# Attention scores as float32 products on 32-row groups instead of split operands stacked through DRAM

## The chip, the cores and the metric

The kernel runs on one core of a Trainium2 chip. Its metric is the device time of one execution in microseconds. The engines of the core have short names in the profile: PE is TensorE's matmul, PEld its weight load, DVE is VectorE, ACT is ScalarE, POOL is GpSimd, and SP is SyncE, whose queue issues the DMAs. A matmul multiplies a stationary operand (loaded by a weight load, up to 128 rows by 128 columns) by a moving operand of up to 512 columns and writes into PSUM, which has eight banks of 512 float32 columns for each of 128 partitions.

## The reference

Four layers follow each other on x (2 sequences of 1024 tokens, 512 wide), each added to its input: a gated recurrence, a feed-forward layer with ternary weights, an attention, and the same feed-forward layer again. The change lies in the attention. Cut to what matters, it is:

```python
B, T, D = x.shape                      # 2, 1024, 512
d = D // H                             # H = 16 heads of 32
q1 = _split_heads(x @ Wq1, H)
q2 = _split_heads(x @ Wq2, H)
k = _split_heads(x @ Wk, H)
v = _split_heads(x @ Wv, H)
q = jnp.concatenate([q1, q2], axis=1)
k2 = jnp.repeat(k, 2, axis=1)
v2 = jnp.repeat(v, 2, axis=1)
scores = jnp.einsum('bhqd,bhkd->bhqk', q, k2) * scale
scores = jnp.where(causal, scores, jnp.finfo(scores.dtype).min)
p = jax.nn.softmax(scores, axis=-1)
y = jnp.einsum('bhqk,bhkd->bhqd', p, v2)
y1, y2 = (y[:, :H], y[:, H:])
lam = jax.nn.sigmoid(x @ Wlam).transpose(0, 2, 1)[..., None]
y = y1 - lam * y2
```

There are 32 query heads, each two of which share a key head. A score is a product over only 32 numbers. The queries of a later token see only earlier ones.

## The kernel before

The attention of a sequence is worked off in **pairs** (line 665): two key heads (e = 0, 1) with one of their two query heads each (the parity `par`). The list `pairs` runs over the sequence b, the group g of four key heads, the half p of the group, and the parity; there are 32 pairs. `project` (L708 to L738) makes, for one group and one kind (kinds 0 and 1: queries of the two parities, kind 2: keys), the product of 512 tokens with the weights, 128 rows = 4 heads x 32. ScalarE writes its rounded high part into `parts` (L724, L728), VectorE the low part (L725, L729), both float32r, and eight DMAs write them to a scratch tensor in DRAM (L738). `load_stacks` reads, two pairs ahead, what a head needs: `ks` has the keys' high part twice and low part twice, `qs` has high, low, high, low, each 32 rows, so that one fp32r matmul over 128 rows adds up all four partial products of a score (L750, L754).

Every score is made twice. `maxima_step` (L785) makes scores with queries on the partitions (tile `s`, L798); VectorE adds the causal mask on the diagonal (L804) and takes the negated maximum of each row (L808). `split_maxima` splits the maxima into three bf16 pieces on GpSimd, and `turn_maxima` turns them with four transposes (tile `mt`, L836) and a VectorE copy (L838). `weights_step` (L843) makes scores again with keys on the partitions (tile `t`, L858), adds the maxima by a bf16 matmul of three rows (L865), and ScalarE takes the exponential into `pr` (L873); on the diagonal GpSimd zeroes what is masked (L876). `weigh` multiplies the weights with the values and a column of ones (tile `y`, L895), in float32, head 0 to the partitions 0 to 63 and head 1 to 64 to 127.

A pair has six steps. TensorE's order is written out by hand in the loop at the end of the attention: in each step first the four products `t` of two (query block, key tile) units and two heads, and their four maxima products; then `y` of the two units of the step before; then what `beside` lists for that step (transposes of the maxima, projections of the next group, normalisation, the output products); and then the step of maxima of the next pair. The units' widths are 512, 384, 256, 128 columns for the first query block and four times 512, then 512, 384, 256, 128 for the second. The banks come from a ring of seven (`ring_bank`), taken in order; a bank is free once its readers of seven banks ago are done: ScalarE for `t`, VectorE for `s`, both for `pq` of a projection, VectorE for `mt`. The list `max_banks` says which products of `s` share a bank: 20 banks a pair, in steps of 4, 4, 3, 3, 3 and 3.

Before the first pair the queries, keys and stacks of its group are made, then `lambdas` and the first maxima with the products of the values between them.

Of the kernel before, what the change touches and what calls it, by code (L numbers as in the profile page):

```python
# [10 lines left out]
F32 = mybir.dt.float32  # L11
F32R = mybir.dt.float32r
# [30 lines left out]
def kernel(  # L43
# [571 lines left out]
    with ExitStack() as s:  # L615
# [5 lines left out]
        ps_ring = s.enter_context(  # L621
            tc.tile_pool(name="b_ring", bufs=7, space=bass.MemoryType.PSUM, reuse_waits="tile")
        )
        kd = s.enter_context(tc.tile_pool(name="b_dram", bufs=2, space=bass.MemoryType.DRAM))

        def ring_bank(name, dtype=F32):
            return ps_ring.tile(
# [39 lines left out]
            (b, g, p, par)  # L667
            for b in range(NT // SEQ) for g in range(NG) for p in range(2) for par in range(2)
        ]
        scratch, stacks, nmax, lams, totals, shares, factors = {}, {}, {}, {}, {}, {}, {}  # L670

        def load_weights(b, g):
            w = b_b.tile([P, NKC, 3 * P], F32, tag="w_qk", name=f"w_qk{b}_{g}")
# [37 lines left out]
        def project(b, g, kind, e, w):  # L711


            n = f"{b}_{g}_{kind}"
            po = ring_bank(f"pq{n}_{e}")
            for k in range(NKC):
                nc.tensor.matmul(  # L717
                    po, w[:, k, ts(kind, P)], xts[b][:, k, ts(e, BLK)],
                    start=(k == 0), stop=(k == NKC - 1),
                )  # L720
            parts = b_p.tile([P, 2, BLK], F32R, tag="parts", name=f"parts{n}_{e}", bufs=2)
            hi, lo = parts[:, 0, :], parts[:, 1, :]
            if kind == 2:
                nc.scalar.copy(hi, po)  # L724
                nc.vector.tensor_sub(lo, po, hi.bitcast(F32))  # L725
            else:
                scale = 1.0 / math.sqrt(HD)
                nc.scalar.mul(hi, po, scale)  # L728
                nc.vector.scalar_tensor_tensor(  # L729
                    lo, po, scale, hi.bitcast(F32), ALU.mult, ALU.subtract  # L730
                )
            if e == 0:

                scratch[b, g, kind] = kd.tile([4, 2, HD, SEQ], F32, tag=f"sc{kind}", name=f"sc{n}")
            sc = scratch[b, g, kind]
            for r in range(2):
                for i in range(4):
                    nc.sync.dma_start(  # L738
                        out=sc[i, r, :, ts(e, BLK)], in_=parts[ts(i, HD), r, :].bitcast(F32)
                    )  # L740

        def load_stack(b, g, kind, i):


            n = f"{b}_{g}_{kind}_{i}"
            sc = scratch[b, g, kind]
            if kind == 2:
                st = b_a.tile([P, SEQ], F32R, tag="ks", name=f"ks{n}", bufs=4)
                for r in range(4):
                    nc.sync.dma_start(out=st[ts(r, HD)].bitcast(F32), in_=sc[i, r // 2])  # L750
            else:
                st = b_d.tile([P, SEQ], F32R, tag="qs", name=f"qs{n}", bufs=6)
                for r in range(2):
                    nc.sync.dma_start(  # L754
                        out=st[ts(r, 2 * HD)].bitcast(F32),
                        in_=sc[i].rearrange("e d n -> (e d) n"),
                    )
            stacks[b, g, kind, i] = st

        def load_stacks(pair):  # L760
            b, g, p, par = pair
            for e in range(2):
                if par == 0:
                    load_stack(b, g, 2, 2 * p + e)
                load_stack(b, g, par, 2 * p + e)

        def operands(pair, e):
            b, g, p, par = pair
            i = 2 * p + e
            return stacks[b, g, 2, i], stacks[b, g, par, i], 4 * g + i  # L770

        def name(pair):
            return "_".join(map(str, pair))

        max_banks = [
            [(0, 0, 128, (0, 1)), (1, 0, 256, (0, 1)), (2, 0, 384, (0,)), (2, 0, 384, (1,))],
            [(j, 0, 512, (e,)) for j in (3, 4) for e in range(2)],
            [(4, 512, 128, (0, 1)), (5, 0, 512, (0,)), (5, 0, 512, (1,))],  # L780
            [(5, 512, 256, (0, 1)), (6, 0, 512, (0,)), (6, 0, 512, (1,))],
            [(6, 512, 384, (0,)), (6, 512, 384, (1,)), (7, 0, 512, (0,))],
            [(7, 0, 512, (1,)), (7, 512, 512, (0,)), (7, 512, 512, (1,))],
        ]

        def maxima_step(pair, step):


            if step == 0:
                nmax[pair] = b_a.tile(  # L790
                    [P, 2, NQ, 2], F32, tag="nmax", name=f"nmax{name(pair)}", bufs=2
                )
            for i, (j, first, nk, heads) in enumerate(max_banks[step]):
                po = ring_bank(f"s{name(pair)}_{step}_{i}")[:, : len(heads) * nk]
                po = po.rearrange("p (e n) -> p e n", n=nk)
                for x, e in enumerate(heads):
                    ks, qs, _ = operands(pair, e)
                    nc.tensor.matmul(  # L798
                        po[:, x, :], qs[:, ts(j, P)], ks[:, first : first + nk],
                        start=True, stop=True,  # L800
                    )
                if first + nk == (j + 1) * P:
                    diagonal = po[:, :, nk - P :]
                    nc.vector.tensor_tensor(  # L804
                        diagonal, diagonal,
                        causal.unsqueeze(1).to_broadcast([P, len(heads), P]), ALU.add,
                    )
                nc.vector.tensor_reduce(  # L808
                    nmax[pair][:, first // BLK, j, heads[0] : heads[-1] + 1], po,
                    AX.X, ALU.max, negate=True,  # L810
                )

        turned = {}
        n_maxima = [0]
# [29 lines left out]
        def weights_step(pair, step):  # L844

            made, banks = [], {}
            for u in (2 * step, 2 * step + 1):
                qb, kb = units[u]  # L850
                lo = max(0, kb - qb * QB) * P
                made.append((u, kb, lo, BLK - lo, kb >= qb * QB))
            for u, kb, lo, nq, _ in made:
                for e in range(2):
                    ks, qs, _ = operands(pair, e)
                    banks[u, e] = ring_bank(f"t{name(pair)}_{u}_{e}")
                    q0 = (qb + 1) * BLK - nq
                    nc.tensor.matmul(  # L858
                        banks[u, e][:, :nq], ks[:, ts(kb, P)], qs[:, q0 : q0 + nq],
                        start=True, stop=False,  # L860
                    )
            for i, (u, kb, lo, nq, _) in enumerate(made):
                for e in range(2):
                    rows = slice(64 * i + 32 * e, 64 * i + 32 * e + 3)
                    nc.tensor.matmul(  # L865
                        banks[u, e][:, :nq], ones[rows], turned[pair, qb][rows, lo:],
                        start=False, stop=True,
                    )
            steps = []
            for u, kb, lo, nq, diagonal in made:  # L870
                pr = b_a.tile([P, 2, BLK], F32, tag="pr", name=f"pr{name(pair)}_{u}", bufs=4)
                for e in range(2):
                    nc.scalar.activation(pr[:, e, :nq], banks[u, e][:, :nq], AF.Exp)  # L873
                if diagonal:

                    nc.gpsimd.affine_select(  # L876
                        out=pr[:, :, :P], in_=pr[:, :, :P], compare_op=ALU.is_ge, fill=0.0,
                        base=0, pattern=[[0, 2], [1, P]], channel_multiplier=-1,
                    )
                steps.append((pair, u, pr))  # L880
            return steps

        def weigh(pair, u, pr):
# [7 lines left out]
            y = outs[pair]  # L891
            last = kb == (qb + 1) * QB - 1
            for e in range(2):
                h = operands(pair, e)[2]
                nc.tensor.matmul(  # L895
                    y[64 * e : 64 * e + 64, lo:],
                    all_values[:, HV * (NH * kb + h) : HV * (NH * kb + h) + 64],
# [77 lines left out]
        for n, pair in enumerate(pairs):  # L975
            b, g, p, par = pair
            following = pairs[n + 1] if n + 1 < len(pairs) else None
            if following:
# [1 line left out]
                at(n, 3, turn_maxima, following, 0)  # L980
                at(n + 1, 0, split_maxima, following, 1)
                at(n + 1, 1, turn_maxima, following, 1)
            if n + 2 < len(pairs):
                at(n, 1, load_stacks, pairs[n + 2])

            nb, ng = divmod(4 * b + g + 1, NG)
            if p == 0 and nb < NT // SEQ:
                def part(kind, e, nb=nb, ng=ng):
                    return lambda: project(nb, ng, kind, e, held["w", nb, ng])
                if par == 0:  # L990
                    at(max(n - 1, 0), 0, lambda nb=nb, ng=ng: hold(("w", nb, ng), load_weights, nb, ng))
                    for t, kind, e in ((1, 2, 0), (2, 2, 1), (4, 0, 0), (5, 0, 1)):
                        at(n, t, part(kind, e))
                else:
                    for t, e in ((2, 0), (4, 1)):
                        at(n, t, part(1, e))

            if g == 2 and p == 1 and b + 1 < NT // SEQ:
                if par == 0:
                    at(n, 0, normal_stats, b + 1)  # L1000
                for t in range(4):
                    at(n, 1 + t, normalise, b + 1, 4 * par + t, ring_bank)
            if g == 3 and p == 1 and b + 1 < NT // SEQ:
                if par == 0:
                    at(n, 0, lambda b=b: hold(("v", b + 1), load_values, b + 1))
# [29 lines left out]
        for kind in (2, 0):  # L1035
            for e in range(2):
                project(0, 0, kind, e, w0)
        load_stacks(pairs[0])
        for e in range(2):
            project(0, 0, 1, e, w0)  # L1040
        load_stacks(pairs[1])
        lambdas(0)
        for step in range(STEPS):
            maxima_step(pairs[0], step)
# [98 lines left out]
```

## Time and profile before

| what | value |
|---|---|
| time before, median of 3 runs | 2176.9 us (2176.82 to 2177.41) |
| profiled execution, its own time | 2177.11 us |
| its span | 2175.3 us |
| granted TensorE clock, mean | 0.995 |
| matmul records and weight loads | 9072 each |
| L858 `t`, float32r, 768 records | 198.4 us busy, mean 357 ns |
| L798 `s`, float32r, 768 records | 206.9 us busy, mean 391 ns |
| L895 `y`, float32, 1536 records | 291.6 us busy, mean 501 ns |
| L717 `pq`, float32, 384 records | 175.8 us busy, mean 603 ns |
| DMA `sc<-parts` / `qs<-sc` / `ks<-sc` | 384 of 64 KB / 128 of 256 KB / 128 of 128 KB |

A float32 matmul stands in the trace as two records, a float32r or bf16 one as a single one. [...] a slot, from the start of one record to the start of the next, is the better measure of what a matmul costs TensorE. In a line of the timeline the columns are the start in us, the length from the first start to the last end in us, engine, line, operation, output <- inputs, the shape of the first record and the number of records; brackets give the idle time before it and what ended it.

### The profile page before, as it was taken

The numbers are of one execution on the slowest core, as the hardware profiler recorded it, in microseconds if no ns is written. First come the engines' busy times: TensorE is split into PE (matmuls) and PEld (weight loads), VectorE is DVE, ScalarE is ACT, GpSimd is POOL, SyncE is SP. The second block draws the span as 40 slices with busy tenths as digits, with TensorE's granted clock in tenths as the row PEclk, the third lists the DMA queues.
The fourth block names the chain that finished last, engine by engine and source line by source line (L and its number), as shares of the span: only waits on it lengthen the run. The fifth ranks groups of instructions, "written<-read, shape, count | busy, mean of one in ns | idle before, by whom it ended". The sixth has DMA issues, their size and how long they took to land.

```text
span 2175.3 us, 26073 instructions
## 1 busy us (share of the span) xinstructions
PE 2122.4 (98%) x9072; PEld 1273.5 (59%) x9072; DVE 1126.2 (52%) x2056; ACT 837.3 (38%) x1592; POOL 448.1 (21%) x808
## 2 busy tenths in 40 slices
PE   8999999999999999999999999999999999999998
PEld 3444444688888844555555454454545547888887
DVE  4767676533443235565656574565656763333322
ACT  4344343234334322343444332243434533343433
POOL 0312123122122220111111112121212221222222
PEclk9999999999999999999999999999999999999999
DMA  6111211600000144343434341244443223000000
GB/s 251 58 58 58 88 58 73 246 1 1 1 1 1 35 105 106 98 112 87 121 83 119 76 123 41 73 104 106 104 105 88 64 83 160 0 20 20 1 20 20
DMA packets 77874, 161.41 MB, mean 74 GB/s; under 512 B 19376, under 2 KB 27568, under 8 KB 77744
## 3 DMA queue, kind: packets, MB, share of 16 engines
q1 hardware_dynamic: 77744, 159.75, 25.1%
q8 instruction: 73, 1.20, 0.2%
q14 instruction: 57, 0.47, 0.1%
HBM read 109.08 MB, written 41.94 MB: 69 GB/s over the span
## 4 chain that ended last, share of the span: by engine, by line
PE 86%; DVE 4%; DMA 4%; ACT 2%; SPq 2%; issue 2%; POOL 0%; DVEq 0%; ACTq 0%; POOLq 0%
PE y L895 11%; PE g L511 11%; PE u L511 11%; PE f_out L532 11%; PE t L858 6%; PE s L798 5%; PE ag L260 5%; PE kv L260 5%; PE pq L717 4%; PE pq L260 3%; PE pv L689 3%; PE a_out L408 3%; PE b_out L956 2%; DMA qs<-sc 2%; PE t L865 2%
## 5 line engine op out<-in xcount | busy, mean ns | idle before, releaser
L873 ACT ACTIVATE pr<-t 128x512 f32<-128x512 f32 (+3 forms) x768 | 314.8, 497 | 368.6 <-PE t L865 364.8
L808 DVE TENSOR_REDUCE nmax<-s 128x1 f32<-128x512 f32 (+3 forms) x640 | 369.7, 627 | 54.6 <-PE s L798 54.5
L895 PE MATMUL y<-pr,val 128*64 128x512 f32 (+3 forms) x1536 | 291.6, 501 | 0.8 <-POOL maxima L827 0.8
L526 POOL TENSOR_TENSOR ssq<-ssq,sq 128x512 f32<-128x512 f32 x120 | 155.9, 1299 | 602.5 <-ACT sq L525 602.5
L517 DVE TENSOR_TENSOR h<-h,u 128x512 f32<-128x512 f32 x128 | 88.0, 688 | 362.5 <-PE u L511 356.4
L511 PE MATMUL g<-xs,w 128*128 128x512 f32 x1024 | 261.8, 397 | 0.9 <-ACT xs L461 0.7
L532 PE MATMUL f_out<-w,hs 128*128 128x512 f32 x1024 | 257.7, 394 | 0.3 <-DVE hs L520 0.3
L511 PE MATMUL u<-xs,w 128*128 128x512 f32 x1024 | 257.0, 393 | 0.0
L876 POOL TENSOR_SCALAR_AFFINE_SELECT pr<-pr 128x256 f32<-128x256 f32 x256 | 101.4, 408 | 593.6 <-ACT pr L873 593.3
L858 PE MATMUL t<-qs,ks 128*128 128x512 f32 (+3 forms) x768 | 198.4, 357 | 22.1 <-DVE parts L729 9.6
L511 PEld LDWEIGHTS u<-xs,w 128*128 128x128 f32 x1024 | 192.9, 188 | 43.6
L532 PEld LDWEIGHTS f_out<-w,hs 128*128 128x128 f32 x1024 | 191.6, 188 | 43.9 <-DVE hs L520 1.1
L804 DVE TENSOR_TENSOR s<-s,causal 128x128 f32<-128x128 f32 (+1 forms) x384 | 115.3, 336 | 195.3 <-PE s L798 195.3
L511 PEld LDWEIGHTS g<-xs,w 128*128 128x128 f32 x1024 | 190.5, 188 | 43.9 <-ACT xs L461 0.9
L798 PE MATMUL s<-ks,qs 128*128 128x512 f32 (+3 forms) x768 | 206.9, 391 | 6.2 <-DMA sc<-parts 3.9
L858 PEld LDWEIGHTS t<-qs,ks 128*128 128x128 f32 x768 | 139.2, 188 | 78.2 <-issue 20.8
L717 PE MATMUL pq<-b_xt,w_qk 128*128 128x512 f32 x384 | 175.8, 603 | 0.0
L519 ACT CAST hs<-h 128x512 fp32r<-128x512 f32 x128 | 79.4, 621 | 237.5 <-DVE h L517 237.5
L895 PEld LDWEIGHTS y<-pr,val 128*64 128x64 f32 x1536 | 93.3, 136 | 120.2 <-issue 86.1
L516 ACT ACTIVATE h<-g 128x512 f32<-128x512 f32 x128 | 76.6, 598 | 224.0 <-PE g L511 223.9
L798 PEld LDWEIGHTS s<-ks,qs 128*128 128x128 f32 x768 | 115.0, 190 | 69.4 <-issue 58.6
L520 DVE TENSOR_TENSOR hs<-h,hs 128x512 fp32r<-128x512 f32 x128 | 88.6, 692 | 83.1 <-ACT hs L519 83.1
(151 smaller groups left out, 2145.5 us busy)
## 6 DMA issues: line engine op xcount, KB each, us to landing
qs<-sc SPq DMA_DIRECT2D x128, 256.0 KB, 4.9
w<-w_kept SPq DMA_DIRECT2D x32, 768.0 KB, 8.9
sc<-parts SPq DMA_DIRECT2D x384, 64.0 KB, 1.7
ks<-sc SPq DMA_DIRECT2D x128, 128.0 KB, 4.0
w_kept<-w SPq DMA_DIRECT2D x16, 768.0 KB, 3.2
w<-in_w_gu_dram SPq DMA_DIRECT2D x32, 256.0 KB, 2.8
share<-ys SPq DMA_DIRECT2D x128, 64.0 KB, 2.0
w_in<-in_w_in_t_dram SPq DMA_DIRECT2D x5, 1024.0 KB, 11.0
```

Of the source, the lines that this page charges most:

```text
L260: nc.tensor.matmul(po, w[:, k, ts(c, P)], xt[:, k, :], start=(k == 0), stop=(k == NKC - 1))
L511: nc.tensor.matmul(po, ws[f][:, part, ts(k, P)], xs[:, e, k, :], start=(k == 0 and e == 0), stop=(k == NKC - 1 and e == 1),)
L526: nc.gpsimd.tensor_add(ssq, ssq, sq)
L532: nc.tensor.matmul(po[j], hp[:, e, ts(j, P)], ws[f][:, 2, :], start=(f == 0 and e == 0), stop=(f == NF - 1 and e == 1),)
L717: nc.tensor.matmul(po, w[:, k, ts(kind, P)], xts[b][:, k, ts(e, BLK)], start=(k == 0), stop=(k == NKC - 1),)
L798: nc.tensor.matmul(po[:, x, :], qs[:, ts(j, P)], ks[:, first : first + nk], start=True, stop=True,)
L804: nc.vector.tensor_tensor(diagonal, diagonal, causal.unsqueeze(1).to_broadcast([P, len(heads), P]), ALU.add,)
L808: nc.vector.tensor_reduce(nmax[pair][:, first // BLK, j, heads[0] : heads[-1] + 1], po, AX.X, ALU.max, negate=True,)
L858: nc.tensor.matmul(banks[u, e][:, :nq], ks[:, ts(kb, P)], qs[:, q0 : q0 + nq], start=True, stop=False,)
L873: nc.scalar.activation(pr[:, e, :nq], banks[u, e][:, :nq], AF.Exp)
L876: nc.gpsimd.affine_select(out=pr[:, :, :P], in_=pr[:, :, :P], compare_op=ALU.is_ge, fill=0.0, base=0, pattern=[[0, 2], [1, P]], channel_mu ...
L895: nc.tensor.matmul(y[64 * e : 64 * e + 64, lo:], all_values[:, HV * (NH * kb + h) : HV * (NH * kb + h) + 64], pr[:, e, : BLK - lo], start= ...
```

## The change

The split into high and low parts, the scratch in DRAM and the stacks go. `project` keeps what ScalarE writes, in full float32, in a tile `group` in SBUF with two copies of the 128 rows: copy 0 as it comes, and copy 1 with the two halves of 64 rows exchanged, written by two DMAs from SBUF to SBUF for each projection. A pair's two heads are one half of the rows in copy 0 and the other half in copy 1, so each head is there on two groups of 32 rows. `operands(pair, i, e)` gives head e on the rows 32 (2i + e). The score products become float32 matmuls over 32 rows: in `weights_step` unit i of the step uses the half i, so that the four products use four row groups; in `maxima_step` each bank belongs to one head and one row group, three banks of 512 columns a step (18 a pair), filled by one or two products. Reductions are one for a bank whose products are equally long, otherwise one for each product. The projections of the next group move to the steps 1, 3 and 5, three for each of two pairs (before: four and two), and the normalisations of the next sequence to the steps 1 and 3.

```diff
-        kd = s.enter_context(tc.tile_pool(name="b_dram", bufs=2, space=bass.MemoryType.DRAM))
...
-            parts = b_p.tile([P, 2, BLK], F32R, tag="parts", name=f"parts{n}_{e}", bufs=2)
-            hi, lo = parts[:, 0, :], parts[:, 1, :]
+            if e == 0:
+
+                pool = (b_d, b_a, b_p)[kind]
+                groups[b, g, kind] = pool.tile(
+                    [P, 2, SEQ], F32, tag=f"group{kind}", name=f"gr{n}", bufs=2
+                )
+            made = groups[b, g, kind][:, :, ts(e, BLK)]
             if kind == 2:
-                nc.scalar.copy(hi, po)
-                nc.vector.tensor_sub(lo, po, hi.bitcast(F32))
+                nc.scalar.copy(made[:, 0, :], po)
             else:
...
-            if e == 0:
-
-                scratch[b, g, kind] = kd.tile([4, 2, HD, SEQ], F32, tag=f"sc{kind}", name=f"sc{n}")
-            sc = scratch[b, g, kind]
-            for r in range(2):
-                for i in range(4):
-                    nc.sync.dma_start(
-                        out=sc[i, r, :, ts(e, BLK)], in_=parts[ts(i, HD), r, :].bitcast(F32)
-                    )
-
-        def load_stack(b, g, kind, i):
...
+                nc.scalar.mul(made[:, 0, :], po, 1.0 / math.sqrt(HD))
+            for i in range(2):
+                nc.sync.dma_start(out=made[ts(i, 64), 1, :], in_=made[ts(1 - i, 64), 0, :])
+
+        def operands(pair, i, e):
+
             b, g, p, par = pair
-            i = 2 * p + e
-            return stacks[b, g, 2, i], stacks[b, g, par, i], 4 * g + i
+            rows = ts(2 * i + e, HD)
+            return (groups[b, g, kind][rows, int(i != p), :] for kind in (2, par))
...
+        fills = {
+            "a": ([(2, 0, 384), (0, 0, 128)], slice(2, 4)),
+            "b": ([(1, 0, 256), (5, 512, 256)], slice(1, 4, 2)),
+            "c": ([(3, 0, 512)], slice(3, 4)),
+            "d": ([(4, 0, 512)], None),
+            "e": ([(5, 0, 512)], None),
+            "f": ([(6, 512, 384), (4, 512, 128)], slice(2, 4)),
+            "g": ([(6, 0, 512)], None),
+            "h": ([(7, 0, 512)], None),
+            "i": ([(7, 512, 512)], slice(3, 4)),
+        }
         max_banks = [
...
+            [(e, i) + fills[f] for f, e, i in step]
+            for step in (
+                [("a", 0, 1), ("a", 1, 1), ("c", 0, 0)],
+                [("b", 0, 1), ("b", 1, 1), ("c", 1, 0)],
+                [("d", 0, 1), ("d", 1, 1), ("e", 0, 0)],
+                [("f", 0, 1), ("f", 1, 1), ("e", 1, 0)],
+                [("g", 0, 1), ("g", 1, 1), ("h", 0, 0)],
+                [("i", 0, 1), ("i", 1, 1), ("h", 1, 0)],
+            )
         ]
...
+            for x, (e, i, products, diagonal) in enumerate(max_banks[step]):
+                po = ring_bank(f"s{name(pair)}_{step}_{x}")
+                keys, queries = operands(pair, i, e)
+                at_col, places = 0, []
+                for j, first, nk in products:
                     nc.tensor.matmul(
-                        po[:, x, :], qs[:, ts(j, P)], ks[:, first : first + nk],
-                        start=True, stop=True,
+                        po[:, at_col : at_col + nk], queries[:, ts(j, P)],
+                        keys[:, first : first + nk], start=True, stop=True,
                     )
...
+                if len({nk for _, _, nk in places}) == 1:
...
+                else:
+                    for place, col, nk in places:
+                        nc.vector.tensor_reduce(
+                            maxima_of[:, place : place + 1], po[:, col : col + nk],
+                            AX.X, ALU.max, negate=True,
+                        )
...
-            for u, kb, lo, nq, _ in made:
+            for i, (u, kb, lo, nq, _) in enumerate(made):
                 for e in range(2):
-                    ks, qs, _ = operands(pair, e)
+                    keys, queries = operands(pair, i, e)
                     banks[u, e] = ring_bank(f"t{name(pair)}_{u}_{e}")
-                    q0 = (qb + 1) * BLK - nq
                     nc.tensor.matmul(
-                        banks[u, e][:, :nq], ks[:, ts(kb, P)], qs[:, q0 : q0 + nq],
+                        banks[u, e][:, :nq], keys[:, ts(kb, P)],
+                        queries[:, (qb + 1) * BLK - nq : (qb + 1) * BLK],
                         start=True, stop=False,
                     )
...
-            if n + 2 < len(pairs):
-                at(n, 1, load_stacks, pairs[n + 2])
...
-                    for t, kind, e in ((1, 2, 0), (2, 2, 1), (4, 0, 0), (5, 0, 1)):
-                        at(n, t, part(kind, e))
-                else:
-                    for t, e in ((2, 0), (4, 1)):
-                        at(n, t, part(1, e))
+
+                for i in range(3):
+                    at(n, 1 + 2 * i, part((2, 0, 1)[(3 * par + i) // 2], (par + i) % 2))
...
-                    at(n, 1 + t, normalise, b + 1, 4 * par + t, ring_bank)
+                    at(n, 1 + 2 * (t // 2), normalise, b + 1, 4 * par + t, ring_bank)
```

## The prediction

> **What bounds it.** I read the page's busy shares first, then the chain of waits, then TensorE's timeline through attention, then VectorE's and ScalarE's groups there.
>
> ```profile
> PE 2122.4 (98%) x9072; PEld 1273.5 (59%) x9072; DVE 1126.2 (52%) x2056; ACT 837.3 (38%) x1592; POOL 448.1 (21%) x808
> ```
> ```profile
> PE 86%; DVE 4%; DMA 4%; ACT 2%; SPq 2%; issue 2%; POOL 0%; DVEq 0%; ACTq 0%; POOLq 0%
> ```
>
> TensorE is the bound nearly everywhere, so the change is worth what it does to TensorE's slots. The stacks' DMAs cost something at one place only. Attention runs from 775 to about 1772 us. The windows show two kinds of pair: the first line is one without a projection beside it, the second one with four.
>
> ```profile
> 1646.20:1667.60 21.40, 21.29 (x130) 11.63 (x129) 15.15 (x36) 10.76 (x27) 5.20 (x19) 1.00 0.47 111
> 967.40:1004.60 37.20, 36.25 (x173) 18.39 (x169) 18.06 (x40) 15.12 (x34) 6.31 (x23) 1.00 0.42 106
> ```
>
> Columns after the time are PE, PEld, DVE, ACT and POOL busy, clock, DMA. The timeline gives a pair's slots, from one start to the next start (start us, length us):
>
> ```profile
> 1670.43 0.40 PE L836 MATMUL mt<-ident,maxima 128*128 128x128 bf16 x4
> 1670.63 1.18 PE L798 MATMUL s<-ks,qs 128*128 128x512 f32 x4
> 1671.65 1.24 PE L858 MATMUL t<-qs,ks 128*128 128x512 f32 x4
> 1672.82 0.39 PE L865 MATMUL t<-mt_s,ones 3*128 3x512 bf16 x4
> 1673.15 0.87 PE L895 MATMUL y<-pr,val 128*64 128x256 f32 x8
> 1673.95 0.95 PE L798 MATMUL s<-ks,qs 128*128 128x128 f32 x4
> 1674.74 1.18 PE L858 MATMUL t<-qs,ks 128*128 128x512 f32 x4
> 1675.85 0.39 PE L865 MATMUL t<-mt_s,ones 3*128 3x512 bf16 x4
> 1676.18 1.94 PE L895 MATMUL y<-pr,val 128*64 128x512 f32 x8
> ```
>
> Over the six steps of this pair the slots are: t 0.91, 1.02, 1.17, 1.11, 0.91, 0.50 = 5.62; s 0.92, 1.02, 0.79, 0.80, 0.70, 0.81 = 5.04; ones (L865) 1.71; y 8.65; the transposes mt 0.40. Sum 21.4.
>
> **Price of a float32 product.** A projection product of 512 columns shows as two records 0.427 us apart, so 0.854 us: four times the 0.2135 us of one pass; the fp32r products of today start 0.228 us apart. Four times the passes is paid back only if four row groups really run together. L865 already does that, with 3 rows each at rows 0, 32, 64, 96: four 512-column products take a slot of 0.33 us, 0.21 of one pass and 0.11 of drain before y changes the array's shape. No float32 product in row groups is in the trace. The nearest row is y, float32 in two column groups. Its eight records fill four places of 0.427 us, and a look at 1676.1 to 1676.6 alone shows two records in the length of one (a first y record is 0.643 us):
>
> ```profile
> 1676.18 0.65 PE L895 MATMUL y<-pr,val 128*64 128x512 f32 x2
> ```
>
> The source issues head 0's product, two records, and then head 1's. Head 1's first record still starts 7 ns behind head 0's first and ahead of its second. Here a rule speaks against the change: the Trainium skill, "TensorE: Matmul & The Clock Gate", Part 3, says matmuls start and end in strict program order. By it a group's second record would hold back the next group: four products take five records, 2.13 us instead of 0.854. That makes t 10.7 us instead of 4.27 and s some 6.8 us dearer: 13 us in each of about 31 pairs, near 2590 us. The row y contradicts it; I go by the row.
>
> **TensorE after, a pair without projections.**
> - t: four products, four row groups, 0.854 us in four steps, 0.427 in steps 1 and 5 (longest 256 columns): 4.27. The drain before L865 (0.11 each, 0.66 in all) goes, as both use 32-row groups. Against 5.62: -1.35.
> - s: each step is three banks of 512 columns in three row groups: 0.854. An s after y or mt loads its weights in the open, as the first projection after y does (0.533 against 0.427, so +0.106), and after mt there is a drain that was not there (2 x 0.11). 6 x 0.96 + 0.22 = 5.98. Against 5.04: +0.94.
> - L865, y, mt: unchanged.
>
> So -0.41 us, before waits.
>
> **What is late next.** There are seven ring banks, and a step now takes 4 (t) + 3 (s): without a projection or mt, each s bank is the one of the step before, and VectorE must have finished it. Three banks now end together after 0.854 us instead of one each 0.228 us, and a late third bank costs a whole 0.854. VectorE's prices here:
>
> ```profile
> L808 DVE TENSOR_REDUCE nmax<-s 128x1 f32<-128x512 f32 x48 | 31.4, 680 | 4.1 <-PE s L798 4.1
> L808 DVE TENSOR_REDUCE nmax<-s 128x1 f32<-128x384 f32 x16 | 8.1, 546 | 0.0
> L804 DVE TENSOR_TENSOR s<-s,causal 128x128 f32<-128x128 f32 x32 | 7.8, 291 | 6.7 <-PE s L798 6.7
> L804 DVE TENSOR_TENSOR s<-s,causal 128x256 f32<-128x256 f32 x18 | 7.2, 427 | 2.9 <-PE s L798 2.9
> ```
> ```profile
> 1671.60 2.47 DVE L808 TENSOR_REDUCE nmax<-s 128x1 f32<-128x512 f32 x4
> 1673.31 2.07 ACT L873 ACTIVATE pr<-t 128x512 f32<-128x512 f32 x4 [3.38 <-PE t L865]
> ```
>
> Four reductions take 2.47, so back to back one costs 0.60 (0.68 the last); likewise 0.20 and 0.34 for masks of 128 and 256. VectorE starts 0.26 after the columns end, and TensorE restarts 0.15 after VectorE's end.
> - Step 5 to 0: 0.26 + 2 x (0.20 + 0.60) + 0.68 + 0.15 = 2.69. TensorE is back after t 0.854, ones 0.325, y 0.80, weights 0.106 = 2.09. Late by 0.60.
> - Step 1 to 2 (two banks of two triangles, one of one): 0.26 + 2 x (0.34 + 0.60) + 0.20 + 0.68 + 0.15 = 3.17 against 2.09. Late by 1.08.
> - Elsewhere y takes 1.65 to 1.87 or the first two banks came early: nothing.
>
> That is 1.68 a pair. ScalarE's four exps (2.07 us from 0.48 after L865's start) would hold the fourth t bank of steps 1 and 3 by some 0.9 together; they hide in these 1.68 and appear if these go. Today's waits are about 1.15 a pair (t 9216 columns, 4.10 + 0.66 of drains, against 5.62; s 4.10 + 0.64 against 5.04), of which 0.95 is t's fourth bank behind VectorE; 0.2 I can't place and carry over. A pair without projections: -0.41 + 1.68 + 0.2 = +1.5.
>
> **Pairs with projections.** Before 37.1 and 29.5, 66.6 for a group of heads. After: three projections each, ScalarE alone frees their bank (VectorE's low parts, 48 x 0.69 us, go). Each: 21.4 - 0.41 + 0.11 (drain in step 5) + 1.68 + 0.2 = 23.0; two, with 6 x 3.41: 66.5. Nothing, seven times.
>
> **Start.** Pair 0 waits for the trip through DRAM:
>
> ```profile
> 804.30 0.64 PE L798 MATMUL s<-ks,qs 128*128 128x128 f32 x3 [1.13 <-DMA qs<-sc]
> 808.81 1.09 PE L798 MATMUL s<-ks,qs 128*128 128x128 f32 x3 [3.87 <-DMA sc<-parts]
> ```
>
> Both go, -5.0: the exchange is two DMAs behind each projection (a 64 KB one lands in 1.7 us today), over before the 7 us of L704. Later the queue loses 640 issues and gains 96; TensorE doesn't wait for it there, so nothing. VectorE has 22 reductions a pair for 20 and two masks fewer, counted above. The moved normalisations are the same transposes, two to a step instead of one, each freed by one ScalarE copy: nothing.
>
> **Sum.** 17 pairs x 1.5 = 25; the last pair, no s: -1; the opening six s: +1; start -5. +20 us on the profiled execution's 2177.1 (span 2175.3), which is the median's 2176.9 within 0.2: **2197 us**.
>
> **Rivals.**
> 1. *Faster: the third bank isn't late.* Then ScalarE's 0.9 replaces 1.68 (-24 us), and if weights load during y's tail, another 0.64 a pair (-20). 2173 to 2153, taken as 2163. It decides below 1.05 us of waits a pair. For: VectorE is busy 15.15 of 21.40 us, so the waits are order, not load. Against: 4 + 3 banks in 7. 24%.
> 2. *In order by product.* s puts two products on one row group ahead of the next bank (steps 0, 1, 3). If a blocked second product holds what follows, these steps take 2.13, 1.71, 2.13: +3.41, of which staggered ends give back 1.45. +2 x 31 us: 2259. For: y never shows a passing of more than one record. 15%.
> 3. *The rule of strict order*, or row groups that don't run together in float32: 2590 or more. 4%.
> 4. Likeliest, 2197, own range 2182 to 2215: 57%.
>
> Faster by over 0.2% (what this kernel's measurement can tell from no change): 0.24; within: 0.06; slower: 0.70. Range 2157 to 2262: from rival 1 with nearly all of its second part to rival 2; it leaves out rival 3 and the ends beyond.
>
> **What would show it.** t slots near 0.86 and 0.43, L865 near 0.33; s near 0.96 but 1.6 in step 0 and 2.0 in step 2, idle put down to VectorE's reductions; pairs of 22.9. s slots of 2.1 in steps 0 and 3 are rival 2; t slots above 2 are rival 3. Pairs under 21.2 prove me wrong.

## The result, and the profile after

The kernel after takes 2226.2 us (median of 4 runs, 2225.58 to 2228.7) against 2177.1 before: 1.0226 times as long, 95% interval 1.0211 to 1.0241. The direction and the range held, but 49 us were added where 20 were forecast.

The page's busy shares and the chain of waits of the kernel after:

```profile
PE 2186.3 (98%) x10598; PEld 1240.3 (56%) x10608; DVE 1122.3 (50%) x2008; ACT 837.2 (38%) x1592; POOL 446.4 (20%) x808
```
```profile
PE 89%; DVE 5%; POOL 2%; issue 2%; ACT 1%; DMA 0%; SPq 0%; DVEq 0%; ACTq 0%; POOLq 0%
```

The DMAs' 4% and SP's queue have left the chain; GpSimd, which was at nothing, has come in with 2%. The change's 1526 more matmul records carry 64 us more of "busy", but that is the time in which at least one record runs, however many row groups work side by side (the 1536 records of L853, 500 ns each, fill 336.0 us), so it says little. The pairs say more. The windows of one pair without and one with projections (columns as in the prediction: time, then PE, PEld, DVE, ACT, POOL busy, clock, DMA share, GB/s):

```profile
1705.50:1729.30 23.80, 23.47 (x181) 10.73 (x181) 16.09 (x36) 10.80 (x28) 5.23 (x18) 1.00 0.05 12
1647.20:1681.70 34.50, 34.17 (x207) 15.19 (x205) 16.11 (x36) 12.61 (x31) 5.23 (x18) 1.00 0.14 31
```

Measured from pair 0's first copy of `y` (L912 before, L908 after) to its second, and from there on from the second copy of one pair to that of the next, the two traces add up like this:

| stretch | before | after | difference, us |
|---|---|---|---|
| start to pair 0's first copy | 860.1 | 852.9 | -7.2 |
| pairs 0 and 1 | 25.3 + 29.7 | 22.9 + 34.4 | +2.3 |
| 17 pairs without projections (15 of 21.4 before, 12 of 23.8 after) | 21.4 to 23.8 | 23.7 to 27.0 | +42.8 |
| 5 times two pairs with projections | 66.5 | 68.9 | +12 |
| change of sequence (pairs 16 and 17) | 137.0 | 134.6 | -2.4 |
| last pair | 19.2 | 20.4 | +1.2 |
| sum, against 48.3 between the last copies of `y` (1772.6 and 1820.9) | | | +48.7 |

The start did what was forecast. TensorE's timeline there no longer shows a wait ahead of the first scores, and the ten records take 1.08 us to the next slot:

```profile
804.29 1.15 PE L782 MATMUL s<-gr,gr 32*128 32x384 f32 x10
805.37 3.70 PE L688 MATMUL pv<-w_v,b_xt 128*128 128x512 f32 x8
809.00 1.15 PE L782 MATMUL s<-gr,gr 32*128 32x256 f32 x10
```

The loss lies in the pairs. TensorE's timeline through one of them (start, length of the row, bracket: idle before it and who ended it):

```profile
1704.57 1.52 PE L782 MATMUL s<-gr,gr 32*128 32x384 f32 x6
...
1707.39 1.72 PE L891 MATMUL y<-pr,val 128*64 128x512 f32 x8 [0.33 <-POOL pr L872]
1709.04 0.40 PE L832 MATMUL mt<-ident,maxima 128*128 128x128 bf16 x4
1709.37 0.72 PE L782 MATMUL s<-gr,gr 32*128 32x256 f32 x3
1709.40 0.69 PE L853 MATMUL t<-gr,gr 32*128 32x512 f32 x1
...
1711.53 0.87 PE L891 MATMUL y<-pr,val 128*64 128x256 f32 x8
1712.33 2.17 PE L782 MATMUL s<-gr,gr 32*128 32x512 f32 x5
1713.85 0.70 PE L853 MATMUL t<-gr,gr 32*128 32x512 f32 x3
```

Since `s`, `t` and the maxima products now interleave, the useful unit is the segment from the first record of `s` to the next `y`: `s` of one step and `t` and L861 of the next. Two segments are long. The one from 1704.57 lasts 2.82 us and carries a wait for GpSimd at its end. The one from 1712.33 lasts 3.60, and in its first five records alone 1.52 us pass before the next row starts. The other four take 2.15, 2.15, 1.61 and 2.14.

| segment | forecast, from its terms | measured |
|---|---|---|
| `s` of step 5, `t` of step 0 | 2.14 | 2.14 |
| `s` 0, `t` 1 (with 0.60 late) | 2.20 | 2.82 |
| `s` 1, `t` 2 | 2.14 | 2.15 |
| `s` 2, `t` 3 (with 1.08 late) | 3.22 | 3.60 |
| `s` 3, `t` 4 | 2.14 | 2.15 |
| `s` 4, `t` 5 | 1.60 | 1.61 |

What a float32 product costs in row groups was thus forecast to 0.01 us; the two waits were not. VectorE's timeline ahead of both, in the same pair:

```profile
1702.79 0.30 DVE L790 TENSOR_TENSOR s<-s,causal 128x128 f32<-128x128 f32 x1 [1.38 <-PE s L782]
1703.12 0.69 DVE L797 TENSOR_REDUCE nmax<-s 128x1 f32<-128x512 f32 x1
1703.73 0.29 DVE L790 TENSOR_TENSOR s<-s,causal 128x128 f32<-128x128 f32 x1
1704.05 1.29 DVE L797 TENSOR_REDUCE nmax<-s 128x1 f32<-128x512 f32 x2
1705.38 0.17 DVE L818 TENSOR_TENSOR nmax<-nmax 128x8 f32<-128x8 f32 x1
...
1710.54 0.43 DVE L790 TENSOR_TENSOR s<-s,causal 128x256 f32<-128x256 f32 x1 [0.63 <-PE s L782]
1711.00 0.69 DVE L797 TENSOR_REDUCE nmax<-s 128x2 f32<-128x512 f32 x1
1711.61 0.42 DVE L790 TENSOR_TENSOR s<-s,causal 128x256 f32<-128x256 f32 x1
1712.07 0.69 DVE L797 TENSOR_REDUCE nmax<-s 128x2 f32<-128x512 f32 x1
1712.68 0.29 DVE L790 TENSOR_TENSOR s<-s,causal 128x128 f32<-128x128 f32 x1
1713.00 1.89 DVE L797 TENSOR_REDUCE nmax<-s 128x1 f32<-128x512 f32 x3
```

Each mask is followed at once by the reduction of the same bank, which starts only when the mask is wholly done: 0.33 us after it for 128 columns, 0.46 for 256. Before, two masks of two banks stood one behind the other, and the reductions behind both (a row of VectorE's timeline before; the reductions start at 1671.60, 0.40 later):

```profile
1671.20 0.49 DVE L804 TENSOR_TENSOR s<-s,causal 128x128 f32<-128x128 f32 x2
```

From there the forecast took 0.20 and 0.34 a mask. From the first mask at 1702.79 to the end of the third reduction (1704.05 + 1.29 = 1705.34) it took 2.55 us, not 2.28; from 1710.54 to the end of the third bank's reduction, some 1713.69, it took 3.15, not 2.76. The record of `s` that waited for it, the fifth of its row, starts 0.15 later, and TensorE's next row at 1713.85.

The wait that the prediction doesn't have at all is GpSimd's. Its timeline:

```profile
1705.61 0.22 POOL L821 CAST maxima<-nmax 128x8 bf16<-128x8 f32 x1 [3.98 <-DVE nmax L818]
...
1706.78 0.22 POOL L825 COPY maxima<-maxima 128x24 bf16<-128x24 bf16 x1
1706.93 0.77 POOL L872 TENSOR_SCALAR_AFFINE_SELECT pr<-pr 128x256 f32<-128x256 f32 x2
```

The five operations of the split stand ahead of the zeroing of the diagonal weights and wait for VectorE's last maxima (L818, 1705.38). So VectorE's lateness reaches `y` a second time, by way of GpSimd. On the page, the idle time before L891 is 10.6 us, all of it put down to L872; before it was 0.8.

The theory from this: in each of about 31 pairs 0.27 us (step 5 to 0) and 0.38 (step 1 to 2) from the masks' place in VectorE's order, and some 0.37 from GpSimd's order, 1.0 in all, make the 29 us between forecast and result. The rivals: that row groups in float32 are dearer in themselves, or that it is the banks' and steps' arrangement (projections, lengths) and not these two orders.

### The profile page after: what moved, and what is told of

Its sections match the earlier page's. It is cut to its first block, busy times and chain, and to the rows that moved or that the text cites. A ratio compares the mean times of both kernels' runs of the same rounds, so it can differ in the third digit from the quotient of the medians.

```text
span 2224.7 us, 27920 instructions
## 1 busy us (share of the span) xinstructions
PE 2186.3 (98%) x10598; PEld 1240.3 (56%) x10608; DVE 1122.3 (50%) x2008; ACT 837.2 (38%) x1592; POOL 446.4 (20%) x808
## 4 chain that ended last, share of the span: by engine, by line
PE 89%; DVE 5%; POOL 2%; issue 2%; ACT 1%; DMA 0%; SPq 0%; DVEq 0%; ACTq 0%; POOLq 0%
PE y L891 11%; PE g L511 11%; PE u L511 11%; PE f_out L532 10%; PE s L782 9%; PE pq L716 8%; PE t L853 5%; PE kv L260 4%; PE ag L260 4%; PE pq L260 3%; PE pv L688 3%; PE a_out L408 3%; DVE nmax L797 2%; PE b_out L952 2%; PE t L861 1%
## 5 line engine op out<-in xcount | busy, mean ns | idle before, releaser
L853 PE MATMUL t<-gr,gr 32*128 32x512 f32 (+3 forms) x1536 | 336.0, 500 | 2.2 <-DVE mt_s L834 1.4
L797 DVE TENSOR_REDUCE nmax<-s 128x1 f32<-128x512 f32 (+1 forms) x448 | 293.9, 685 | 42.9 <-PE s L782 35.4
L891 PE MATMUL y<-pr,val 128*64 128x512 f32 (+3 forms) x1536 | 290.2, 499 | 10.6 <-POOL pr L872 10.6
L782 PE MATMUL s<-gr,gr 32*128 32x512 f32 (+3 forms) x1536 | 287.3, 518 | 0.0
L790 DVE TENSOR_TENSOR s<-s,causal 128x256 f32<-128x256 f32 (+1 forms) x320 | 116.5, 373 | 262.0 <-PE s L782 260.3
L891 PEld LDWEIGHTS y<-pr,val 128*64 128x64 f32 x1536 | 93.3, 136 | 196.3 <-issue 156.1
L782 PEld LDWEIGHTS s<-gr,gr 32*128 32x128 f32 x1536 | 127.8, 183 | 122.3 <-issue 55.4
L853 PEld LDWEIGHTS t<-gr,gr 32*128 32x128 f32 x1536 | 150.0, 184 | 51.5 <-issue 43.0
L872 POOL TENSOR_SCALAR_AFFINE_SELECT pr<-pr 128x256 f32<-128x256 f32 x256 | 99.5, 407 | 377.4 <-ACT pr L869 377.4
L861 PE MATMUL t<-mt_s,ones 3*128 3x512 bf16 (+3 forms) x768 | 153.8, 323 | 0.0
```

The source lines that it names most:

```text
L782: nc.tensor.matmul(po[:, at_col : at_col + nk], queries[:, ts(j, P)], keys[:, first : first + nk], start=True, stop=True,)
L790: nc.vector.tensor_tensor(tiles, tiles, causal.unsqueeze(1).to_broadcast([P, len(products), P]), ALU.add,)
L797: nc.vector.tensor_reduce(maxima_of[:, lo : hi + 1 : max(hi - lo, 1)], po.rearrange("p (a n) -> p a n", n=places[0][2]), AX.X, ALU.max, ne ...
L853: nc.tensor.matmul(banks[u, e][:, :nq], keys[:, ts(kb, P)], queries[:, (qb + 1) * BLK - nq : (qb + 1) * BLK], start=True, stop=False,)
L861: nc.tensor.matmul(banks[u, e][:, :nq], ones[rows], turned[pair, qb][rows, lo:], start=False, stop=True,)
L891: nc.tensor.matmul(y[64 * e : 64 * e + 64, lo:], all_values[:, HV * (NH * kb + h) : HV * (NH * kb + h) + 64], pr[:, e, : BLK - lo], start= ...
```

## Experiments

Every time is a median, with its ratio to the kernel before on the same chip. The medians there were 2177.5 for no masks, masks first, even steps and light steps; 2178.5 for masks twice, the kernel before without masks and the three together; 2179.1 for GpSimd's order and the last two runs.

**No masks, and the masks twice.** The causal add is all that is taken out, or doubled.

```diff
-                if diagonal:
+                if False:
```

> The changed kernel without VectorE's causal additions before the maxima: the mask is left out of the maxima (the weights themselves are still masked), nothing on TensorE changes. Theory (VectorE's three banks a step are handed back late, because each reduction waits for the full length of its mask): the chain behind a step falls from 2.91 us (step 5) and 3.5 us (step 1) to 0.2 + 0.6 + 0.6 + 0.68 + 0.15 = 2.23 us against TensorE's return after 2.09, so 0.93 and 1.5 us of waits a pair and GpSimd's 0.33 nearly go; ScalarE's fourth t bank, hidden until now, gives back up to 0.9. A pair without projections falls from 23.8 to about 22.1, the whole by some 45 to 55 us, to 2170 to 2182. Rival (the float32 products, their weight loads in the open and the drains cost it on TensorE itself): VectorE isn't on the path, 2220 or more.

2175.65 us, 0.9994 (0.9985 to 1.0002): 50 us less than after, as much as the change had cost. Pairs take 22.1 and 32.7. In TensorE's timeline the segment with 3.60 has become 2.58 and the one with 2.82 has become 2.16, of which GpSimd's part stays:

```profile
1659.76 1.72 PE L891 MATMUL y<-pr,val 128*64 128x512 f32 x8 [0.34 <-POOL pr L872]
```

```diff
+                if diagonal:
+                    nc.vector.tensor_tensor(
+                        tiles, tiles,
+                        causal.unsqueeze(1).to_broadcast([P, len(products), P]), ALU.add,
+                    )
```

> The changed kernel with each causal addition made twice (the second one changes nothing that matters to the maximum). Nothing on TensorE changes. Theory: each further mask stands between the columns and its reduction, 2 x 0.3 us behind step 5, 2 x 0.46 + 0.33 behind step 1, and the chains behind steps 0 and 3 become late too: 1.9 to 3 us a pair, +59 to +93 us, 2285 to 2319. Rival: VectorE is busy half of the time only, so 120 us more of it spread over attention costs little, 2226 to 2240.

2316.4, 1.0637 (1.0618 to 1.0655). The mean granted clock was 0.981 here against 0.998, so the size isn't clean; but in a pair at full clock the segments behind step 1 (3.60 to 4.11), step 5 (2.82 to 3.35) and `s` 4 with `t` 5 (1.61 to 2.27) grew while the ones at 2.15 stayed. Together the two runs show that VectorE's handing back of the banks is what TensorE pays for, but not yet whether by the amount of its work or by its order.

**The masks taken out of the kernel before.**

```diff
-                if first + nk == (j + 1) * P:
+                if False:
```

> The kernel before without VectorE's causal additions before the maxima: the mask is left out of the maxima, as in the run without masks of the changed kernel. Theory: today's 0.95 us of waits a pair, t's fourth bank behind VectorE, shrink, -0.4 to -0.9 in each of 31 pairs: 2149 to 2165. The changed kernel without masks took 2175.7, so the row groups by themselves, with VectorE out of the way on both sides, would be 10 to 27 us dearer than the stacked products. Rival (VectorE costs the kernel before nothing): 2175 to 2178, and the row groups by themselves cost the same as the stacks.

2141.2, 0.983 (0.9818 to 0.9843): 37 us less, more than expected. A plain pair shrinks by only 0.4 (21.4 to 21.0), but two pairs with projections by 3.6 (66.5 to 62.9). So the kernel before carried mask waits too, most of them beside the projections. Against this run the row groups without masks are 34 us dearer. A plain pair shows the difference (22.1 and 21.0) in its segments: `s` 0 with `t` 1 +0.31 (GpSimd's 0.34 lies in it), `s` 2 with `t` 3 +0.35, the other four -0.21 to +0.20, and the two transposes' slots 0.33 each for 0.21, as `s` after them changes the array's shape.

**Masks first, then reductions.** Nothing is left out; VectorE does all masks of a step and then its reductions, in written order.

```diff
+            filled = []
...
+                filled.append((po, places))
+            for po, places in filled:
...
-                    maxima_step(pairs[n + 1], step)
+                    with tc.manual_schedule(engines={mybir.EngineType.DVE}):
+                        maxima_step(pairs[n + 1], step)
```

> The changed kernel with VectorE's order in a step written out: the masks of all three banks, then all reductions. Same instructions. Theory: masks then cost 0.20 and 0.34 us each instead of 0.335 and 0.46 to 0.54; the third bank is back 0.27 us earlier behind step 5 and 0.37 behind step 1: -0.6 us in each of 31 pairs, about -19, to 2207. Rival (cost on TensorE itself): no change, 2224 to 2228. If GpSimd's masking behind its split of the maxima is a wait of its own, it stays, and the gain is 0.6 a pair and no more.

2206.6, 1.0137 (1.0122 to 1.0152): 20 us less than after, with the same instructions. VectorE's timeline behind step 5:

```profile
1711.18 0.50 DVE L791 TENSOR_TENSOR s<-s,causal 128x128 f32<-128x128 f32 x2 [1.38 <-PE s L783]
1711.59 1.88 DVE L800 TENSOR_REDUCE nmax<-s 128x1 f32<-128x512 f32 x3
```

From the first mask to the end of the third reduction 2.29 us pass: the forecast's 2.28. The 0.65 a pair that this order was held to cost, times 31, is 20. Behind step 1 the segment falls from 3.60 to 3.27. This is the size of the masks' term, shown by itself.

**GpSimd: the split behind the zeroing.** One tiny copy makes the split of the second half wait for the zeroed weights.

```diff
+            if half and "pr" in held:
+                nc.gpsimd.tensor_copy(rest[:, 0, :], held["pr"][:, 1, 0:2])
...
+                held["pr"] = made[-1][2]
```

> The changed kernel with GpSimd's order turned round in step 0: one tiny copy ties the split of the second half of the maxima to the zeroing of the diagonal weights, so that the five operations of the split come after the two zeroings and not ahead of them. Theory (GpSimd is a wait of its own, 0.33 us ahead of y in step 1 of pairs without projections, and also in those whose projection comes later than that y): 0.33 less in each of 31 pairs, -10 us, or -6 if only the 17 pairs without projections have it: 2216 to 2221. Rival (that idle time is only VectorE's lateness seen from another engine): no change, 2225 to 2228.

2214.4, 1.0163 (1.0149 to 1.0177): 12 us less than after, somewhat more than expected. `s` 0 with `t` 1 goes from 2.82 to 2.42. GpSimd's timeline has the zeroing ahead of four of the split's five operations, and TensorE's `y` no bracket before it:

```profile
1696.36 0.76 POOL L874 TENSOR_SCALAR_AFFINE_SELECT pr<-pr 128x256 f32<-128x256 f32 x2
...
1697.45 0.21 POOL L824 TENSOR_TENSOR mrest<-nmax,maxima 128x8 f32<-128x8 f32 x1
```
```profile
1697.60 1.73 PE L893 MATMUL y<-pr,val 128*64 128x512 f32 x8
```

0.40 times 31 is 12. This and the run before make 32 us, and the forecast was missed by 29; the two edits were not tried together without others.

**Projections in the even steps.** They are set into the steps whose banks are late, to cover the two waits.

```diff
-                    at(n, 1 + 2 * i, part((2, 0, 1)[(3 * par + i) // 2], (par + i) % 2))
+                    at(n, 2 * i, part((2, 0, 1)[(3 * par + i) // 2], (par + i) % 2))
```

> The changed kernel with the projections of the next group in steps 0, 2 and 4 instead of 1, 3 and 5. Same instructions. Theory: the two late banks are in steps 0 and 2, between y and s; 3.4 us of projection there cover them, in the 14 pairs that have projections: 0.93 + 1.5 + 0.33 us less each, -34 to -38 us, to 2188 to 2192; pairs without projections stay at 23.8. Rival (cost on TensorE itself): a projection is as long in one step as in another, 2222 to 2230.

2210.6, 1.0154 (1.0139 to 1.0169): a gain of 16 where 36 were expected. In pairs with projections the two long segments do shrink (2.88 to 1.62, 3.60 to 2.14), but a wait comes up in step 1, which was at 2.15 and is now 2.82. TensorE's timeline in such a pair:

```profile
1637.19 0.40 PE L832 MATMUL mt<-ident,maxima 128*128 128x128 bf16 x4
1637.62 1.40 PE L782 MATMUL s<-gr,gr 32*128 32x256 f32 x5
1638.33 0.69 PE L853 MATMUL t<-gr,gr 32*128 32x512 f32 x1
```

and VectorE's last reduction of step 0 there:

```profile
1637.48 0.68 DVE L797 TENSOR_REDUCE nmax<-s 128x1 f32<-128x512 f32 x1
```

The transposes take a ring bank of their own, so a bank of step 1 is the third one of step 0, free at 1638.16; TensorE's next row starts 0.17 later. In after the projection stood just there and covered it. The expectation had counted only the covered waits. From pair 15 to pair 17, around the change of sequence, 2.5 us were lost as well.

**Light steps ahead of short ones.** The same 18 banks in another order of steps, with the split and the turn a step later, so that the step with the heavy triangles isn't followed by a short cover.

```diff
                 [("a", 0, 1), ("a", 1, 1), ("c", 0, 0)],
-                [("b", 0, 1), ("b", 1, 1), ("c", 1, 0)],
                 [("d", 0, 1), ("d", 1, 1), ("e", 0, 0)],
+                [("b", 0, 1), ("b", 1, 1), ("c", 1, 0)],
                 [("f", 0, 1), ("f", 1, 1), ("e", 1, 0)],
-                [("g", 0, 1), ("g", 1, 1), ("h", 0, 0)],
                 [("i", 0, 1), ("i", 1, 1), ("h", 1, 0)],
+                [("g", 0, 1), ("g", 1, 1), ("h", 0, 0)],
...
-                at(n, 2, split_maxima, following, 0)
-                at(n, 3, turn_maxima, following, 0)
+                at(n, 3, split_maxima, following, 0)
+                at(n, 4, turn_maxima, following, 0)
...
-            if step == 1:
+            if step == 2:
```

> The changed kernel with the fills of the banks in another order of steps: the steps that are followed by the short y (1 and 5, 0.80 us) get three banks without mask, those with two triangles go to steps 2 and 3, ahead of the long y (1.87 us); the first half of the maxima is split and turned one step later. Same products. Theory: the chain behind steps 1 and 5 is 2.23 against 2.09 (0.14 late); behind step 2 3.5 against 3.15 (0.35), behind step 4 2.9 against 2.4 (0.5): about 1.1 us of waits instead of 2.4 in pairs without projections and almost none in those with; ScalarE's fourth t bank comes back with up to 0.6. -30 to -45 us, to 2181 to 2196. Rival (cost on TensorE itself): 2222 to 2230.

2194.6, 1.0079 (1.0062 to 1.0096), inside what was expected; pairs 23.0 and 33.0. The sum holds better than its terms. Behind step 4 the forecast's 0.5 is there (`s` 5 with `t` 0 at 2.63 for 2.14), and `s` 2 with `t` 3 at 2.75 has the 0.6 expected of ScalarE's bank. But the 0.35 behind step 2 isn't there (`s` 3 with `t` 4 at 2.15), and behind step 0 stands 0.55 that wasn't forecast (`s` 1 with `t` 2 at 2.70).

**All three together.** Masks first, this order of banks, and the projections in the steps 0, 2 and 5.

```diff
-                    at(n, 1 + 2 * i, part((2, 0, 1)[(3 * par + i) // 2], (par + i) % 2))
+                    at(n, (0, 2, 5)[i], part((2, 0, 1)[(3 * par + i) // 2], (par + i) % 2))
```

> The changed kernel with all three edits: masks ahead of the reductions, the fills without mask ahead of the short y, and the projections in the steps 0, 2 and 5, where the two single edits still show waits. Theory: pairs without projections come down to 22.1, as without masks (waits left: ScalarE's fourth t bank and GpSimd's masking), pairs with projections to about 31.7: 17 x 1.7 + 14 x 2.7 = 67 us less than 2226, 2159; 2153 to 2172 as a wait that is covered in one step may come back in the next. Rival (the float32 row groups cost more on TensorE than the stacked products, whatever VectorE does): not under 2175.

2177.9, 0.9996 (0.9988 to 1.0004): a miss, some 6 us above the upper end. The pairs came down (22.3 to 22.5, and 32.0), but pair 16, which holds the second sequence's values and output products of the first, rose from 80.7 to 85.4 us, and the one ahead of it from 27.0 to 29.3.

**And with GpSimd's order.** The run before, with the copy of the GpSimd run, and the projections that stand beside the second sequence's first group back in the steps 1, 3 and 5.

```diff
+                    at(n, (0, 2, 5)[i] if g or not b else 1 + 2 * i, part((2, 0, 1)[(3 * par + i) // 2], (par + i) % 2))
```

> The three edits together, with GpSimd's order turned round as well, and the projections of the first group of the second sequence back in steps 1, 3 and 5, where the run of three together lost some 5 us at the change of sequence. Theory: 2178 - 5 (change of sequence) - 0.3 x 17 (zeroing) = 2168, 2163 to 2172: below the kernel before. Rival (what is covered in one place comes back in another): 2175 to 2180.

2173.3, 0.9971 (0.9961 to 0.9981), a little above what was expected: around the change of sequence (pairs 15 to 17) only 2.6 us came back of the 5. This is with every operation of the kernel after and the tiny copies, 53 us less than after and 0.3% less than before. Pairs take 22.2 and 32.0; plain ones are still dearer than before's 21.4, those with projections cheaper than 66.5 for two.

**The same without masks.**

```diff
-                if diagonal:
+                if False:
```

> The best schedule without VectorE's causal additions; the mask is left out of the maxima. It asks what the float32 row groups cost when VectorE is out of the way and the schedule suits them; the kernel before without masks took 2141.2. Theory (row groups are dearer on TensorE by weights in the open after every change of shape, 0.1 us, and drains; 1.1 us a pair without projections between the two kernels without masks): still 10 to 20 us above the kernel before without masks, 2152 to 2162. Rival (only handing back banks made them dearer): 2141 or less.

2168.1, 0.9951 (0.9938 to 0.9965): 5 us less than with masks, where 11 to 21 were expected, and 27 above the kernel before without masks. Two segments stay long. `s` 0 with `t` 1 takes 1.84 for 1.60, and the weights of `y` behind it wait 0.23 for GpSimd's zeroing:

```profile
1653.03 0.23 PEld L896 LDWEIGHTS y<-pr,val 128*64 128x64 f32 x4 [0.23 <-POOL pr L877]
```

`s` 2 with `t` 3 takes 2.75 for 2.14. TensorE's rows and ScalarE's there:

```profile
1657.99 0.85 PE L783 MATMUL s<-gr,gr 32*128 32x256 f32 x3
...
1658.98 1.18 PE L858 MATMUL t<-gr,gr 32*128 32x512 f32 x3
```
```profile
1657.36 2.06 ACT L874 ACTIVATE pr<-t 128x512 f32<-128x512 f32 x4 [3.21 <-PE t L866]
```

ScalarE's fourth exponential ends at 1659.42, and the first record of `t` on the fourth bank starts at 1659.47, inside the second row. This is the hold of the fourth `t` bank behind ScalarE that the prediction named as hidden: with VectorE out of the way it is the longest wait left, 0.61 of a pair. No run took it away, so its size is read from the trace alone.

## Why the prediction was right, and where it failed

- **Four row groups in float32.** Right. The four undisturbed segments came out within 0.01 us of the sum of the terms, weights in the open (0.106) and the missing drain included. Row groups also pass each other: at 1709.37 the timeline has `s`, and 0.03 us later `t`, which the source issues behind all ten records of `s`, on the fourth row group. So the rule of strict order in the Trainium skill, "TensorE: Matmul & The Clock Gate", Part 3, doesn't hold between row groups here. What is passed are records that queue behind others of their own row group; one that waits for its bank isn't passed (last section). With the rule rival 3 and, as the segments behind the steps 1 and 3 are undisturbed, rival 2 fall.
- **The start.** Right in kind: both waits went, and pair 0's first copy came 7.2 us earlier, not 5. The rest wasn't tried by itself; the granted clock from 848 to 860 us was 0.87 before and 1.00 after, and before waited 1.20 us for ScalarE at 846.5.
- **"What is late next".** The mechanism and both places were right, and this is the step whose size failed: the waits of a pair, 0.60 + 1.08 = 1.68 in the prediction, measured 1.22 + 1.46 = 2.68 (the two long segments less their sums without waits, 1.60 and 2.14). Of the 1.00 more, 0.66 is the masks' and 0.34 GpSimd's (the page's 10.6 us before L891, over 31 pairs). Over 31 pairs this makes 31 us, where the whole sum missed by 29. The term 2 x (0.20 + 0.60) measured 2.55 - 0.68 = 1.87 in place of 1.60 behind step 5, and the chain behind step 1 3.15 in place of 2.76, since a mask directly ahead of its own reduction costs its whole length. The price came from a row of before where each mask had another instruction between it and its own reduction. With the masks put first, 20 us were gone.
- **The GpSimd wait** isn't in the prediction, which followed VectorE's and ScalarE's chains and put GpSimd at nothing without a reason. The split waits for the last maximum and has the zeroing behind it in order: 0.33 us a pair by its bracket, and 12 us in all by the run that turned the order round.
- **Plain pairs** cost +2.4 us in place of +1.5, by these terms. **Pairs with projections** were to cost nothing and cost +2.4 for two. The sum there took the same two waits as in plain pairs, so it was off by the same terms.
- **The range.** 2226 lies outside 2182 to 2215, the likeliest case's own range. It lies inside the wide one only because that reaches up to rival 2, whose mechanism didn't come; this is luck.
- **Waits of today.** 1.15 us a pair in all, of which 0.95 were placed on VectorE in plain pairs. The place was wrong: the masks cost a plain pair 0.4 and one with projections 1.8. That their 37 us are 1.2 a pair on the mean, near 1.15, is chance, as the 1.15 was worked out from a plain pair. The 0.95 can't be right as it stands either: all slots of `t` together lie 5.62 - 4.10 - 0.66 = 0.86 above their sum.
- **Rival 1** (faster) needs VectorE to be in time. The run with GpSimd's order gets a part of it by order alone: -6 us against before, not the -14 that this rival stood for. In its plain pairs `s` 2 with `t` 3 stays at 2.75, and the fourth `t` again starts 0.05 behind ScalarE's fourth exponential.

What stays open: the 34 us between the two kernels without masks were not taken apart by a run. In a plain pair, 1.1 us dearer, 0.34 us is GpSimd's by its bracket, 0.24 the transposes' slots, and 0.35 `s` 2 with `t` 3. That last one takes 2.58 for 2.14 in the changed kernel without masks, and its trace puts it down to ScalarE there too:

```profile
1663.89 2.07 ACT L869 ACTIVATE pr<-t 128x512 f32<-128x512 f32 x4 [3.37 <-PE t L861]
```
```profile
1665.56 1.14 PE L853 MATMUL t<-gr,gr 32*128 32x512 f32 x4
```

The fourth exponential ends at 1665.95, and the last of these four records, the first on the fourth bank, starts at 1666.00.

The lowest time of all, 2141.2 us, is the kernel before with the mask left out of the maxima. Any upper bound of the row's scores cancels in a softmax that divides by its own sum, so this is a change worth its own study; but with a bound far above the largest visible score the exponentials become small, and how far that goes on other inputs wasn't tried.

## What to carry to other kernels

Where banks come free together and are needed together, sum the chain of the last one with the producer and consumer of each bank in their real order: an operation that feeds the very next one on its engine (VectorE's masks here) costs its whole length, not its rate. Then ask of every engine that waits for the late result what stands behind its waiting instruction; here a second engine passed the delay on. And moving a cover to one late bank uncovers another, so the ring has to be followed bank by bank before a gain is added up.

## What the hardware showed that was not expected

- On VectorE, two masks of 128 columns on different banks take 0.49 us, one 0.20 behind the other, but a reduction that reads the masked bank starts 0.33 after it (256 columns: 0.34 and 0.46 to 0.54). The order alone, with equal instructions, moved the whole kernel by 20 us.
- A matmul on a free row group passes up to seven earlier records that queue for other row groups: the `t` at 1709.40 starts 0.03 us behind `s`'s first record. It doesn't pass one that waits for its bank. In step 2 the third bank's record of `s` waited until 1713.84, and the first `t` behind it starts 0.01 later, at 1713.85, though one row group has no `s` in this step and ScalarE was done with the four banks of the `t` before at 1713.58:

```profile
1711.52 2.06 ACT L869 ACTIVATE pr<-t 128x512 f32<-128x512 f32 x4 [3.36 <-PE t L861]
```
